# Nine source tiles at a time for the last 53 attention targets

## The chip, the cores and the metric

The kernel runs on one core of a Trainium2 chip. The metric is the device time of one execution in microseconds; the figure of a kernel is the median of its runs. Its engines are named as in the profile: PE (TensorE, with PEld for its weight loads), DVE (VectorE), ACT (ScalarE), POOL (GpSimd) and SP (SyncE, which here issues DMAs).

## The reference

Two graph layers on 3125 nodes with 256 features, each of a graph convolution, a mixing step and an expert step. The change lies in the expert step of the first layer, where a graph attention decides how a node's experts are weighed. Cut to that:

```
h = (x @ W_gat).reshape(M, HEADS, NUM_EXPERTS)        # M = 3125, 4 heads, 4 experts
src = concatenate([edge_index[0], loops])             # edges and a loop at each node
dst = concatenate([edge_index[1], loops])
a_src = (h * att_src).sum(-1)
a_dst = (h * att_dst).sum(-1)
e = leaky_relu(a_src[src] + a_dst[dst], negative_slope=0.2)
e_max = segment_max(e, dst)
ee = exp(e - e_max[dst])
denom = segment_sum(ee, dst)
alpha = ee / (denom[dst] + 1e-16)
agg = segment_sum(h[src] * alpha[:, :, None], dst)    # then layer norm, top 2, softmax
```

## The kernel before

The edges are first made into a dense matrix of counts C in DRAM: row is the target, column the source, and the value is how often the edge occurs. The attention then works on full tiles. For a source tile of 128 nodes (on the partitions) and a group of targets (along the columns) it makes the term exp(e - e_max) for each of four heads, multiplies it by the count, and TensorE sums over the sources with the values h as weights.

Nodes lie in NT = 25 tiles of 128; the last has LAST = 53. Sources are taken tile by tile. Targets are taken in groups of eight tiles (`wide`, L1058): groups 0, 1 and 2 have 1024 targets, group 3 has only the 53 of the last tile. The loop (L1272) takes group 3 first, then 0, 1, 2, and each has 25 steps, one for each source tile.

Before that, a loop over the targets (L1000 to L1039) finds the maxima with VectorE, and from them makes up nine rows of values for each target (`pq`), which are transposed and written to DRAM (`pq_d`, L1039). Rows 0 and 1 hold the slope-1 value of heads 2 and 3 less the maximum. Rows 2, 3 and 6, 7 hold the slope-0.2 value of heads 0, 1 and 2, 3 less the maximum. Rows 4, 5 and 8 hold 0.8 times the target's own value, for heads 0, 1 and 2.

One step has these parts:

- `logits` (L1065): at a group's first step it loads seven rows of `pq_d`, spread over all partitions (`pqb`, L1072), and lets PE spread two more into PSUM (`pb`, L1081). At every second step it loads the counts of two source tiles (`cd`, L1088 or, for the 53, L1092; two buffers). Then the terms before the exponential, in a buffer `ex` of four: for heads 0 and 1 (and head 2 at odd steps) a Relu on ACT (L1099, L1102) and an add on POOL (L1100, L1103), for the others one operation on DVE with `pb` from PSUM (L1105).
- `terms` (L1108): four Exps on ACT, one for each head, with the source's part as a bias (L1116); transposes of the counts on PE into PSUM (`ct`, L1121, two buffers); one DVE operation on all heads, min with 1 and product with the count (L1123).
- `summed` (L1126): four products on PE into `pa` (L1135), a PSUM tile of which there is one buffer.

The loop keeps `logits` one step ahead of `terms`, and `summed` one piece behind. When a group is done, `weighed` (L1138) copies `pa` (L1148), divides, does the layer norm and the choice of experts, and adds the experts' results to `xs`; it is a generator of which the loop takes a piece at a time during the next group, and its small operations run on POOL for groups 3, 0 and 1. The instructions are written in this order, and a planner then decides the order on each engine by priority and readiness, so that some stand elsewhere than they were written; within an engine they run in the planned order.

Of the kernel before, what the change touches and what calls it, by code (L numbers as in the profile page):

```python
# [8 lines left out]
F32 = mybir.dt.float32  # L9
# [8 lines left out]
P = 128  # L18
# [25 lines left out]
HELD = 8  # L44
PACE = 1.05
COLS = 32
MOSTW = 192
CLR = 3056
BEFORE = 4096.0
# [36 lines left out]
def tile_gps(ctx: ExitStack, tc: tile.TileContext, a, out):  # L86
# [43 lines left out]
    A1 = dram.tile([P * CLR * 25], BF16, name="A1")  # L130
    C2 = dram.tile([P * CLR * 25], F32, name="C2")
    as_d = dram.tile([4, N], F32, name="as_d")
    pq_d = dram.tile([9, N], F32, name="pq_d")
    y_d = dram.tile([NT, P, 4, D], F32, name="y_d")
    slots = dram.tile([EX * CAP + SLOT, XW], F32, name="slots")
    hT_d = dram.tile([P, 4, N], F32, name="hT_d")
# [153 lines left out]
    def split_rows(r):  # L290

        return [(0, r)] if r % 16 == 0 else [(0, r - r % 16), (r - r % 16, r)]
# [614 lines left out]
    with ExitStack() as st:  # L907
# [39 lines left out]
        with ExitStack() as st2:  # L947
            ps = st2.enter_context(tc.tile_pool(name="ps_gat", bufs=1, space=PSUM))
            xp = st2.enter_context(tc.tile_pool(name="experts", bufs=1))
            beside0 = experts()  # L950
            ap = st2.enter_context(tc.tile_pool(name="gatp", bufs=1))
            wgat = ap.tile([P, 2, 16], F32, name="wgat", tag="wgat")
            nc.sync.dma_start(wgat, a["w_gat"])
            for g in range(NG):
                ts = tiles_of(g)
                r = rows_of(ts[-1])
                nx = work_rows(len(ts), r)
                normed(nx, [xs[:r, t, :] for t in ts], r, scalar=True)
                hT = work.tile([P, 2, 512], F32, name="hT", tag="hT")
                transposed(ps, hT, nx, r)  # L960
                nc.sync.dma_start(xf_d[:, :, 512 * g:512 * g + cols_of(g)], hT[:, :, :cols_of(g)])
                ph = ps.tile([P, 512], F32, name="ph", tag="pa", bufs=2)
                for j, t in enumerate(ts):
                    for k in range(2):
                        T.matmul(ph[:r, 16 * j:16 * j + 16], lhsT=hT[:, k, j * P:j * P + r], rhs=wgat[:, k, :],
                                 start=(k == 0), stop=(k == 1))
                V.tensor_copy(hg[:r, ts[0]:ts[-1] + 1, :], ph[:r, :16 * len(ts)].rearrange("p (t h) -> p t h", h=16))
            for nm in ("att_src", "att_dst"):
                tmp = ap.tile([P, NT, 16], F32, name="atmp", tag="atmp")
                V.tensor_tensor(tmp, hg, bcast(nm)[:, None, :].to_broadcast([P, NT, 16]), op=OP.mult)  # L970
                V.tensor_reduce(att[nm].rearrange("p t h -> p (t h)"), tmp.rearrange("p t (h e) -> p (t h) e", e=4),
                                axis=AX.X, op=OP.add)

            for g in range(NG):
                p = ps.tile([P, 512], F32, name="tr", tag="tr", bufs=2)
                for j, t in enumerate(tiles_of(g)):
                    r = rows_of(t)
                    T.transpose(p[:4, j * P:j * P + r], att["att_src"][:r, t, :], ident[:r, :r])
                n = cols_of(g)
                asT = ap.tile([4, 512], F32, name="asT", tag="rowsT", bufs=2)  # L980
                S.activation(asT[:, :n], p[:4, :n], AF.Copy)
                nc.sync.dma_start(as_d[:, 512 * g:512 * g + n], asT[:, :n])
            V.tensor_scalar(as8[:, :, 0:2], att["att_src"][:, :, 0:2], 0.8, None, op0=OP.mult)
            V.tensor_scalar(as8[:, :, 2:4], att["att_src"][:, :, 2:4], -0.8, None, op0=OP.mult)
            V.tensor_scalar(as6[:, :, 0:2], att["att_src"][:, :, 0:2], 0.2, None, op0=OP.mult)
            V.tensor_copy(as6[:, :, 2:4], att["att_src"][:, :, 2:4])
            V.tensor_scalar(as2[:, :, 0:1], att["att_src"][:, :, 2:3], 0.8, None, op0=OP.mult)
            V.tensor_scalar(as2[:, :, 1:2], att["att_src"][:, :, 2:3], 0.2, None, op0=OP.mult)
            for _ in range(2):
                next(beside0, None)  # L990
            asb = ap.tile([P, 4, N], F32, name="asb", tag="asb")
            for h in range(4):
                nc.sync.dma_start(asb[:, h, :], as_d[h:h + 1, :].to_broadcast([P, N]))
            edge_stack.close()
            tc.no_sync_barrier()
            rp = ap
            ap = st2.enter_context(tc.tile_pool(name="gat0", bufs=1, reuse_waits="tile"))


            for g in range(NG):  # L1000
                ts = tiles_of(g)
                for t in ts:
                    r = rows_of(t)
                    cnt = ap.tile([P, N], F32, name="cnt", tag="cnt", bufs=2)
                    for q0, q1 in split_rows(r):
                        nc.sync.dma_start(cnt[q0:q1], C22[t * P + q0:t * P + q1, :])
                    for i, (c0, c1) in enumerate(((0, MID), (MID, N))):
                        w = c1 - c0
                        pen = ap.tile([P, MID], F32, name="pen", tag="pen", bufs=2)
                        S.activation(pen[:r, :w], cnt[:r, c0:c1], AF.Relu, scale=MASKED, bias=big[:r])  # L1010
                        for h in range(4):
                            junk = ap.tile([P, MID], F32, name="am", tag="am", bufs=1)
                            V.tensor_tensor_reduce(out=junk[:r, :w], in0=asb[:r, h, c0:c1], in1=pen[:r, :w], scale=1.0,  # L1013
                                                   scalar=-3.0e38, op0=OP.subtract, op1=OP.max,
                                                   accum_out=zz[:r, i, t, h:h + 1])
                    next(beside0, None)

                r, n = rows_of(ts[-1]), cols_of(g)  # L1020
                z0, z1 = (zz[:r, i, ts[0]:ts[-1] + 1, :] for i in range(2))
                zg, ad = z[:r, ts[0]:ts[-1] + 1, :], att["att_dst"][:r, ts[0]:ts[-1] + 1, :]
                m = small.tile([P, 4, 4], F32, name="gm", tag="gm")
                pq = small.tile([P, 4, 9], F32, name="pq", tag="pq")
                k = len(ts)
                V.tensor_tensor(zg, z0, z1, op=OP.max)
                V.tensor_tensor(zg, zg, ad, op=OP.add)
                V.scalar_tensor_tensor(m[:r, :k], zg, 0.2, zg, op0=OP.mult, op1=OP.max)
                V.tensor_tensor(pq[:r, :k, 0:2], ad[:, :, 2:4], m[:r, :k, 2:4], op=OP.subtract)
                V.scalar_tensor_tensor(pq[:r, :k, 2:4], ad[:, :, 0:2], 0.2, m[:r, :k, 0:2], op0=OP.mult, op1=OP.subtract)  # L1030
                V.tensor_scalar(pq[:r, :k, 4:6], ad[:, :, 0:2], 0.8, None, op0=OP.mult)
                V.tensor_scalar(pq[:r, :k, 8:9], ad[:, :, 2:3], 0.8, None, op0=OP.mult)
                V.scalar_tensor_tensor(pq[:r, :k, 6:8], ad[:, :, 2:4], 0.2, m[:r, :k, 2:4], op0=OP.mult, op1=OP.subtract)
                p = ps.tile([P, 512], F32, name="tr", tag="tr", bufs=2)
                for j in range(k):
                    T.transpose(p[:9, j * P:j * P + r], pq[:r, j, :], ident[:r, :r])
                pqT = rp.tile([9, 512], F32, name="pqT", tag="rowsT", bufs=2)
                S.activation(pqT[:, :n], p[:9, :n], AF.Copy)
                nc.sync.dma_start(pq_d[:, 512 * g:512 * g + n], pqT[:, :n])  # L1039
            for _ in beside0:  # L1040
                pass

        with ExitStack() as st2:
            ps = st2.enter_context(tc.tile_pool(name="ps_gat1", bufs=1, space=PSUM))
            ap = st2.enter_context(tc.tile_pool(name="gat1", bufs=1, reuse_waits="tile"))
            def ptile():
                return ps.tile([P, 512], F32, name="ct", tag="ct", bufs=2)
# [78 lines left out]
            def summed(g, s, ex, c, m, state):  # L1126
                ts = wide[g]
                r, rt = rows_of(s), rows_of(ts[-1])
                n = P * (len(ts) - 1) + rt
                if s == 0 and c == 0:  # L1130
                    state["sums"] = ps.tile([P, 1024], F32, name="pa", tag="pa", bufs=1)
                pa = state["sums"]
                for h in range(4):
                    at = 20 * s + 5 * h
                    T.matmul(pa[32 * h:32 * h + 32, c:c + m], lhsT=hgp[:r, at:at + 32], rhs=ex[:r, h, c:c + m],  # L1135
                                 start=(s == 0), stop=(s == NT - 1))

            def weighed(g):  # L1138

# [129 lines left out]
                if want in (None, where):  # L1269
                    want = next(done, "none")  # L1270

            for x in [(g, s) for g in (3, 0, 1, 2) for s in range(NT)] + [None]:  # L1272
                if x:
                    ahead.append(logits(*x, state))
                    if len(ahead) == 1:
# [561 lines left out]
```

## Time and profile before

| | us |
|---|---|
| median of 3 runs | 5010.62 (5009.96 to 5020.74) |
| the profiled execution | 5011.07 |
| its span, first to last instruction | 5009.2 |
| the 53 targets: first Relu to the copy of their sums | 2990.5 to 3037.8 |
| the three full groups: to the copy of the last sums | to 3591.7 |

The profile is of one execution. Busy times are sums over an engine's instructions. In an order of time each row gives the start, the length, the engine, the line, the operation with output and inputs, and in brackets how long the engine was idle before it and what ended that. "x4" means four like instructions merged into a row. In a row of a line or a tile, three durations stand for minimum, median and maximum in ns. In a table by stage each engine has its busy us and its count of instructions, then follow the granted clock of PE, the share of DMA time, and GB/s.

The granted PE clock is 0.50 in both the stretch 2985 to 2991 and the stage of the 53 targets, and 0.76 to 0.94 in the stretches of the full groups from 3042 on. POOL does nothing for 391.1 us before its first add of the attention at 2990.96.

### The profile page before, as it was taken

The numbers are of one execution on the slowest core, as the hardware profiler recorded it, in microseconds if no ns is written. First come the engines' busy times: TensorE is split into PE (matmuls) and PEld (weight loads), VectorE is DVE, ScalarE is ACT, GpSimd is POOL, SyncE is SP. The second block draws the span as 40 slices with busy tenths as digits, with TensorE's granted clock in tenths as the row PEclk, the third lists the DMA queues.
The fourth block names the chain that finished last, engine by engine and source line by source line (L and its number), as shares of the span: only waits on it lengthen the run. The fifth ranks groups of instructions, "written<-read, shape, count | busy, mean of one in ns | idle before, by whom it ended". The sixth has DMA issues, their size and how long they took to land. (4 is left out here: it accounts for less than half of the span.)

```text
span 5009.2 us, 50021 instructions
## 1 busy us (share of the span) xinstructions
PE 3962.3 (79%) x16580; PEld 2289.4 (46%) x16671; DVE 3195.5 (64%) x8087; ACT 1516.3 (30%) x2412; POOL 2723.9 (54%) x1835
## 2 busy tenths in 40 slices
PE   1467788778866786788979955576789998999998
PEld 1244455444543454454456632232345444544477
DVE  7978887888799879511149987989882031321331
ACT  0312132113211131130034449998640030000033
POOL 2578888888888888877750007888520030010033
PEclk6768887888877787889979977887999999999999
DMA  9934443444322322236565533332382212222266
GB/s 331 290 54 69 76 70 43 73 76 63 47 26 17 34 9 22 4 28 119 65 168 191 184 126 100 103 98 72 96 258 70 80 47 65 68 63 61 68 169 164
DMA packets 446884, 472.05 MB, mean 94 GB/s; under 512 B 213042, under 2 KB 354139, under 8 KB 441558
## 3 DMA queue, kind: packets, MB, share of 16 engines
q1 hardware_dynamic: 249418, 455.15, 29.0%
q0 software_dynamic: 197184, 13.47, 12.2%
q8 instruction: 139, 2.28, 0.2%
q14 instruction: 143, 1.16, 0.1%
HBM read 338.77 MB, written 130.63 MB: 94 GB/s over the span
## 5 line engine op out<-in xcount | busy, mean ns | idle before, releaser
L404 POOL DMA_INDIRECT A<-lowa,keya x782 | 1213.8, 1552 | 368.5 <-issue 222.0
L404 POOL DMA_INDIRECT C<-valb,keyb x512 | 793.7, 1550 | 219.8 <-issue 146.1
L1100 POOL TENSOR_TENSOR ex<-ex,pqb 128x1024 f32<-128x1024 f32 (+3 forms) x200 | 366.8, 1856 | 463.6 <-ACT ex L1099 463.4
L350 DVE SCALAR_TENSOR_TENSOR junk<-kr,keya,w_before 128x640 bf16<-128x640 f32 (+2 forms) x729 | 603.5, 828 | 12.2 <-DMA kr<-keys_a 2.0
L393 DVE SCALAR_TENSOR_TENSOR junk<-kr,keyb,w_before 128x1024 bf16<-128x1024 f32 (+1 forms) x390 | 496.4, 1273 | 12.9 <-DMA kr<-keys_b 6.3
L195 PE MATMUL tr<-ident,rows 128*128 128x128 f32 (+1 forms) x500 | 108.4, 371 | 492.6 <-ACT rows L181 486.4
L229 PE MATMUL mm<-hT,w 128*128 128x512 f32 (+1 forms) x896 | 420.2, 634 | 17.2 <-ACT hT L197 17.2
L760 PE MATMUL ag<-chb,Hb 128*128 128x512 bf16 (+1 forms) x1752 | 412.1, 385 | 17.2 <-DMA chb<-A 15.0
L760 PE MATMUL ag<-chb,xb 128*128 128x512 bf16 (+3 forms) x1907 | 398.0, 365 | 15.8 <-DMA chb<-A 13.2
L1013 DVE CUSTOM_DVE_ANT_0 am<-asb,pen 128x1664 f32<-128x1664 f32 (+3 forms) x200 | 357.3, 1786 | 54.0 <-ACT pen L1010 43.7
L717 PE MATMUL o<-w,hid 128*128 128x256 f32 (+1 forms) x1600 | 384.3, 393 | 0.0
L1135 PE MATMUL pa<-ex,hgp 128*32 128x512 f32 (+3 forms) x1400 | 204.5, 664 | 201.6 <-DVE ex L1123 200.4
L1123 DVE SCALAR_TENSOR_TENSOR ex<-ex,ct 128x2048 f32<-128x2048 f32 (+3 forms) x175 | 345.8, 2007 | 27.6 <-ACT ex L1116 14.1
L1116 ACT ACTIVATE ex<-ex,as 128x1024 f32<-128x1024 f32 (+3 forms) x400 | 345.0, 932 | 4.9 <-DVE ex L1105 4.9
L717 PEld LDWEIGHTS o<-w,hid 128*128 128x128 f32 (+1 forms) x1600 | 297.0, 190 | 79.4 <-issue 37.5
L1366 POOL DMA_INDIRECT slots<-rb,r_ati x50 | 50.0, 1000 | 513.6 <-DVE rb L1359 406.9
L232 ACT ACTIVATE hid<-mm,fm 128x512 f32<-128x512 f32 (+1 forms) x336 | 211.0, 631 | 363.5 <-PE mm L229 362.1
L195 PEld LDWEIGHTS tr<-ident,rows 128*128 128x128 f32 (+1 forms) x500 | 68.6, 180 | 538.7 <-ACT rows L181 521.1
L229 PEld LDWEIGHTS mm<-hT,w 128*128 128x128 f32 x896 | 192.0, 233 | 237.6 <-issue 190.4
L760 PEld LDWEIGHTS <-xb 128*128 128x128 bf16 (+1 forms) x2100 | 183.2, 97 | 231.9 <-issue 22.6
L760 PEld LDWEIGHTS <-Hb 128*128 128x128 bf16 (+1 forms) x2100 | 184.1, 99 | 226.6 <-issue 33.2
L181 ACT ACTIVATE rows<-xs,ln_nmr,rs_y 128x256 f32<-128x256 f32 (+1 forms) x225 | 118.9, 592 | 494.8 <-DVE ln_nmr L174 475.5
(441 smaller groups left out, 6653.5 us busy)
## 6 DMA issues: line engine op xcount, KB each, us to landing
C<-zero SPq DMA_DIRECT2D x25, 1528.0 KB
cnt<-C SPq DMA_DIRECT2D x24, 1562.5 KB
cd<-C SPq DMA_DIRECT2D x36, 1024.0 KB
kr<-keys_b SPq DMA_DIRECT2D x64, 512.0 KB
f1w<-in_f_w_dram SPq DMA_DIRECT2D x56, 512.0 KB
slots<-blank SPq DMA_DIRECT2D x15, 1820.0 KB
kr<-keys_a SPq DMA_DIRECT2D x48, 512.0 KB
kr<-keys_a SPq DMA_DIRECT2D x69, 320.0 KB
```

What stands on the lines that cost most here:

```text
L229: T.matmul(ph[:, :n], lhsT=w1[:, k, hb * P:(hb + 1) * P], rhs=xT[:, k, :n], start=(k == 0), stop=(k == 1))
L232: S.activation(h[:, :n], ph[:, :n], AF.Gelu, bias=bias[hb])
L350: V.scalar_tensor_tensor(junk[:, :k * P], self.kr[:, at:at + k * P], key[:, c + j:c + j + 1], self.w_before[:, u:u + k * P], op0=OP.is_equ ...
L393: V.scalar_tensor_tensor(out, kk, key[:, c + j:c + j + 1], by, op0=OP.is_equal, op1=OP.mult, accum_out=more[:, j:j + 1] if i else self.val ...
L404: s = G.indirect_dma_start(out=self.flat, out_offset=bass.IndirectOffsetOnAxis(ap=self.idx[:, c:c + 1], axis=0), in_=(self.val if self.low ...
L717: T.matmul(po[:r], lhsT=hid[hb][:, j * P:j * P + r], rhs=w2[:, hb, :], start=(hb == 0), stop=False)
L760: T.matmul(acc[fb, g][:, :n], lhsT=Xb[:r, s, i, fb * P:(fb + 1) * P], rhs=ch[:r, at:at + n], start=first, stop=last, skip_group_check=g == ...
L1013: V.tensor_tensor_reduce(out=junk[:r, :w], in0=asb[:r, h, c0:c1], in1=pen[:r, :w], scale=1.0, scalar=-3.0e38, op0=OP.subtract, op1=OP.max, ...
L1100: G.tensor_tensor(e, e, pq[:r, h, :n], op=OP.add)
L1116: S.activation(ex[:r, h, :n], ex[:r, h, :n], AF.Exp, bias=sc)
L1123: V.scalar_tensor_tensor(e4, e4, 1.0, ct[:r, None, :m].to_broadcast([r, 4, m]), op0=OP.min, op1=OP.mult)
L1135: T.matmul(pa[32 * h:32 * h + 32, c:c + m], lhsT=hgp[:r, at:at + 32], rhs=ex[:r, h, c:c + m], start=(s == 0), stop=(s == NT - 1))
```

## The change

The 53 targets leave the loop and get a function of their own, `last_targets`. It takes the source tiles in groups of MANY = 9 (9, 9 and 7) and makes the terms of a group together, with the columns in the order source tile, target. For each head three DVE operations replace Relu, add and L1105: 0.8 times the source's value plus 0.8 times the target's; max with zero plus the target's slope-0.2 row; plus 0.2 times the source's value. The source's value is read from `att_src`, repeated over the 53 columns; the target's rows, `rows4`, are repeated over the source tiles. One Exp without a bias works on all four heads of a group. The counts of all source tiles are loaded in two pieces (of 2048 and 1077 columns) that hold both `cd` buffers until they are transposed. The min and product is one DVE operation a head, in the last group two, since its last source tile has 53 rows. The products on PE are as before. `pq` has ten rows instead of nine (the tenth is head 3's 0.8 row). The loop then starts at group 0, with `weighed(3)` handed to it as the work to be taken in pieces.

```
-                pq = small.tile([P, 4, 9], F32, name="pq", tag="pq")
+                pq = small.tile([P, 4, 10], F32, name="pq", tag="pq")
...
-                V.tensor_scalar(pq[:r, :k, 8:9], ad[:, :, 2:3], 0.8, None, op0=OP.mult)
+                V.tensor_scalar(pq[:r, :k, 8:10], ad[:, :, 2:4], 0.8, None, op0=OP.mult)
...
+            def last_targets():
+
+                n, q0 = LAST, P * (NT - 1)
+                rows4 = ap.tile([P, 8, LAST], F32, name="rows4", tag="rows4")
+                for i, k in enumerate((2, 6, 4, 8)):
+                    nc.sync.dma_start(rows4[:, 2 * i:2 * i + 2, :], pq_d[k:k + 2, q0:N].rearrange("(o k) n -> o k n", o=1)
+                                      .to_broadcast([P, 2, n]))
+                cds = []
+                for c0 in range(0, N, 8 * SRC):
+                    c1 = min(c0 + 8 * SRC, N)
+                    cd = ap.tile([P, 8, SRC], F32, name="cd", tag="cd", bufs=2).rearrange("p j c -> p (j c)")
+                    for p0, p1 in split_rows(n):
+                        nc.sync.dma_start(cd[p0:p1, :c1 - c0], C22[q0 + p0:q0 + p1, c0:c1])
+                    cds.append(cd)
+                state["sums"] = ps.tile([P, 1024], F32, name="pa", tag="pa", bufs=1)
+                pa = state["sums"]
+                for s0 in range(0, NT, MANY):
+                    some = list(range(s0, min(s0 + MANY, NT)))
+                    k = len(some)
+                    ex = ap.tile([P, 4, 1024], F32, name="ex", tag="ex", bufs=4)
+                    e = ex.rearrange("p h n -> p (h n)")[:, :4 * k * n].rearrange("p (h s n) -> p h s n", h=4, n=n)
+                    for h in range(4):
+                        src = att["att_src"][:, s0:s0 + k, h:h + 1].to_broadcast([P, k, n])
+                        w, a8 = (rows4[:, i + h:i + h + 1, :].to_broadcast([P, k, n]) for i in (0, 4))
+                        V.scalar_tensor_tensor(e[:, h], src, 0.8, a8, op0=OP.mult, op1=OP.add)
+                        V.scalar_tensor_tensor(e[:, h], e[:, h], 0.0, w, op0=OP.max, op1=OP.add)
+                        V.scalar_tensor_tensor(e[:, h], src, 0.2, e[:, h], op0=OP.mult, op1=OP.add)
+                    S.activation(e, e, AF.Exp)
+                    ct = ptile()
+                    for j, s in enumerate(some):
+                        r, c = rows_of(s), P * s
+                        T.transpose(ct[:r, j * n:j * n + n], cds[c // (8 * SRC)][:n, c % (8 * SRC):c % (8 * SRC) + r],
+                                    ident[:n, :n])
+                    full = k - (some[-1] == NT - 1)
+                    for r, i0, i1 in ((P, 0, full), (LAST, full, k)):
+                        if i0 < i1:
+                            for h in range(4):
+                                V.scalar_tensor_tensor(e[:r, h, i0:i1], e[:r, h, i0:i1], 1.0,
+                                                       ct[:r, i0 * n:i1 * n].rearrange("p (s n) -> p s n", n=n),
+                                                       op0=OP.min, op1=OP.mult)
+                    for j, s in enumerate(some):
+                        r = rows_of(s)
+                        for h in range(4):
+                            at = 20 * s + 5 * h
+                            T.matmul(pa[32 * h:32 * h + 32, :n], lhsT=hgp[:r, at:at + 32], rhs=e[:r, h, j, :],
+                                     start=(s == 0), stop=(s == NT - 1))
...
-            for x in [(g, s) for g in (3, 0, 1, 2) for s in range(NT)] + [None]:
+            last_targets()
+            done = weighed(3)
+            for x in [(g, s) for g in (0, 1, 2) for s in range(NT)] + [None]:
```

More of the change, by code (lines that the diff above doesn't have):

```diff
@@ L46 @@
 COLS = 32
+MANY = 9
 MOSTW = 192
@@ L132, in tile_gps @@
     as_d = dram.tile([4, N], F32, name="as_d")
-    pq_d = dram.tile([9, N], F32, name="pq_d")
+    pq_d = dram.tile([10, N], F32, name="pq_d")
     y_d = dram.tile([NT, P, 4, D], F32, name="y_d")
@@ L1035, in tile_gps @@
                 for j in range(k):
-                    T.transpose(p[:9, j * P:j * P + r], pq[:r, j, :], ident[:r, :r])
-                pqT = rp.tile([9, 512], F32, name="pqT", tag="rowsT", bufs=2)
-                S.activation(pqT[:, :n], p[:9, :n], AF.Copy)
+                    T.transpose(p[:10, j * P:j * P + r], pq[:r, j, :], ident[:r, :r])
+                pqT = rp.tile([10, 512], F32, name="pqT", tag="rowsT", bufs=2)
+                S.activation(pqT[:, :n], p[:10, :n], AF.Copy)
                 nc.sync.dma_start(pq_d[:, 512 * g:512 * g + n], pqT[:, :n])
```

## The prediction

> **What bounds the kernel now.** I read the page's busy table first, then the stage of the change in the table by stage, then its waits and its order of time, then the costs of single operations by form.
>
> ```profile
> PE 3962.3 (79%) x16580; PEld 2289.4 (46%) x16671; DVE 3195.5 (64%) x8087; ACT 1516.3 (30%) x2412; POOL 2723.9 (54%) x1835
> ```
>
> ScalarE (ACT) is the least busy engine of the whole span, but the attention is another matter. Its second part, 2991 to 3592 us, cut where the group of 53 ends:
>
> ```profile
> core 0: us, PE busy (x) PEld busy (x) DVE busy (x) ACT busy (x) POOL busy (x), PEclk, DMA share, GB/s
> 2991.00:3028.00 37.00, 16.41 (x203) 9.32 (x204) 17.22 (x61) 36.91 (x156) 16.68 (x62) 0.50 0.31 111
> 3028.00:3592.00 564.00, 366.10 (x2052) 140.47 (x2051) 511.53 (x394) 514.13 (x514) 466.90 (x261) 0.84 0.31 98
> ```
>
> In the first row ACT works 36.91 of 37.00 us and VectorE (DVE) 17.22: the 53 targets are bound by ACT. In the second row both stand at 91%, so a lead that one of them alone wins is soon used up. The waits of the first stretch say the same: DVE's L1123 waits for ACT's Exp, 19 times.
>
> ```profile
> DVE ex L1123 <- ACT ex L1116: 7.8, 19, 1.7
> PE ct L1121 <- DMA cd<-C: 3.3, 1, 3.3
> ```
>
> By form, the widths of the 53 and of the full groups:
>
> ```profile
> L1116 ACT ACTIVATE ex<-ex,as x400: 323/1132/1150, 2993.1 to 3583.0; 128x1024 f32<-128x1024 f32 x96, 128x53 f32<-128x53 f32 x32, 53x1024 f32<-53x1024 f32 x4, 53x53 f32<-53x53 f32 x2
> L1123 DVE SCALAR_TENSOR_TENSOR ex<-ex,ct x175: 361/2278/2290, 2994.2 to 3588.2; 128x2048 f32<-128x2048 f32 x144, 128x212 f32<-128x212 f32 x24, 53x2048 f32<-53x2048 f32 x6, 53x212 f32<-53x212 f32 x1
> ```
>
> The minimum is the 53's. An Exp of 53 columns costs 323 ns against 1132 for 1024: 279 ns of it are fixed. 25 tiles with 6.5 ACT instructions each, at 0.23 us apart, are the 37 us. Where the stage ends and what follows:
>
> ```profile
> 2990.53 1.03 ACT L1099 ACTIVATE ex<-pqb,as 128x53 f32<-128x53 f32 x4 [5.22 <-DMA pqb<-pq_d]
> 3034.54 2.47 DVE L1105 SCALAR_TENSOR_TENSOR ex<-pqb,as,pb 128x1024 f32<-128x1024 f32 x2 [5.54 <-PE pb L1081]
> 3042.22 4.48 DVE L1123 SCALAR_TENSOR_TENSOR ex<-ex,ct 128x2048 f32<-128x2048 f32 x2 [0.16 <-ACT ex L1116]
> ```
>
> The mark I measure against is 3042.22, the first L1123 of the first full group (group 0, source tile 0). What that instruction gains, the end should gain: after it 75 equal steps follow, then stages that depend on their end.
>
> [...] 896 elements, both sources in SBUF, 1.09 us (row below[...]). [...]
>
> ```profile
> 18.73 1.09 DVE L278 SCALAR_TENSOR_TENSOR kfa<-sfa,dfa 128x896 f32<-128x896 f32 x1
> ```
>
> [...] The trace shows such a lock. A VectorE operation on 16 elements took 2.47 us and ended with a GpSimd (POOL) add of 2.37 us; a two-SBUF one on 4 elements took 0.64 beside an add of 0.65:
>
> ```profile
> 3088.01 2.47 DVE L1214 TENSOR_SCALAR g_over<-g_diff 53x16 f32<-53x16 f32 x1
> 3088.10 4.67 POOL L1100 TENSOR_TENSOR ex<-ex,pqb 128x1024 f32<-128x1024 f32 x2
> 3660.99 1.30 POOL L732 TENSOR_TENSOR rest<-rows,xb 128x256 f32<-128x256 f32 x2 [0.99 <-ACT xb L731]
> 3661.04 0.64 DVE L174 SCALAR_TENSOR_TENSOR ln_nmr<-ln_mv,rs_y 128x4 f32<-128x4 f32 x1
> ```
>
> The kernel before keeps one operand of L1105 and L1123 in PSUM, so its adds run free. The new operations have both in SBUF. [...]
>
> **The change, part by part.** *Removed:* for the 53, all ACT work (36.9 us), POOL's adds, L1105 and the 25 small L1123; the transposes and the 100 products per source tile and head stay. ACT keeps three Exps of 1908, 1908 and 1484 elements[...], so 32 us of ACT go. The wait of 3.3 us for counts goes too: all counts are asked for at once (0.66 MB) and are needed 8 us later.
>
> *Added on VectorE.* Groups of 9, 9 and 7 source tiles. The A part: three operations per head, 12 a group. [...] Dependent ones in the trace stand 0.03 us more than their duration apart (0.26 for 0.23), independent ones about 0.06 less: 0.66 and 0.55 on average. 24 x 0.66 + 12 x 0.55 = 22.4 us. The B part, min and product, has its counts in PSUM. L1123's 212 elements at 0.38 and 2048 at 2.28 give 1.035 ns each, so 477 at 0.65, 0.59 apart: 8 x 0.59 = 4.7. The last group is 4 of 318 (0.43) and 4 of 53 (0.15): 2.3. Together 29.4 us against 17.2 now. VectorE is the stage's bound then.
>
> *The start.* Four small loads (rows4) in place of one; at 0.38 us an issue the fourth is 1.1 us later on SP's queue, but the first head needs the first and third: I take 2990.8 in place of 2990.53. The four count loads follow, then group 0's rows (3584 KB), issued at 2988.9 now and landed near 3002 by the DMA bars; 2 us later on SP costs nothing before 3003.
>
> *The waits.* B of a group waits for its Exp, behind it in program order the next group's A. But instructions aren't kept in program order: the timeline shows a load of the weighing stage (L1233) at 2947.61, in the maxima loop, and layer-norm steps of the next stage between the last L1123s at 3580. So I take A of the next group into the Exp's time. Only the last Exp [...] has no A left; two L1105 of group 0 (2.5 us) fill it. The end of B: 2990.8 + 29.4 + 2.5 = 3022.7. PE's products take 0.35 us a source tile, and its `pb` for group 0 (3.8 us) can run early, both beside that.
>
> *Brought forward.* ACT and POOL are now free from 3003 on, and ex has four buffers: three groups take three, the fourth goes to tile 0 of group 0; tile 1 takes the first group's once its products are done (about 3006), tile 2 the second's (about 3016). So two, three and two Relus and as many POOL adds can come early; ACT is then far enough ahead that tile 0's Exps are done at 3022. Without interference the mark moves from 3042.2 to 3022.7: 19.5 us.
>
> *The lock.* Each POOL add inside an A part stops VectorE for up to 2.37 us. At least 2 fall there, at most 7. I take 4: two of tile 0, and of tile 1's three two, since its third Relu stands on ACT behind the second Exp, which the delayed A holds up. 4 x 2.37 = 9.5.
>
> *Nothing:* one row more in pq (L1024 to L1038): the same instruction counts. The held count buffers are free by the third group's transposes, before group 0 is in need.
>
> **Sum:** 19.5 - 9.5 = 10.0 us. The profiled execution took 5011.07 (span 5009.2 and 1.9 around it), so 5001.1; against the median 5010.62, 5000.6.
>
> **Rivals.**
> - *Fewer collisions.* POOL loses the lock to back-to-back VectorE, or only tile 0's adds come early: 19.5 less 0 to 4.7, so 4991 to 4996. For it: an add waits as well as VectorE. Against: at 3088 POOL won.
> - *Small gain.* Program order is kept: per group A 7.9, Exp and hand-over 2.0, B 2.4, so 12.3 twice and 10.6: end at 3026; then products 3.0, `pb` 3.8, two L1105 2.5 and an Exp 1.3: mark at 3036.6, gain 5.6, 5005.0. Six or seven adds in the A parts give the same, 2.9 to 5.3. Against the first: the rows moved across stages.
> - *Slower: the second SBUF operand.* [...] It decides once rate and lock together cost over 19.5 us. L278 speaks against the rate, though not with an operand repeated across columns as here.
>
> **Numbers.** Chances: forecast 0.42 (three to five adds, gain 7.6 to 12.4), fewer collisions 0.22, small gain 0.22, slower 0.14. The bound of what can be told from no change is 0.2%, 10.0 us. Faster by more: 0.22 and a bit over half of the forecast's, 0.46. Within: 0.18 + 0.22 + 0.03 = 0.43. Slower by more: 0.11 of the last. The range 4989 to 5016 takes in all cases but most of the last.
>
> **What would show it.** In the changed profile: twelve new VectorE operations a group at 0.65 us ([...] near 3 beside an add is the lock); [...] VectorE's next A inside each Exp (else the second rival); POOL adds of 1024 before the last B, and how many; the first full L1123 near 3032 from an unchanged start of the stage. The forecast is wrong if that mark gains and the end does not, the full groups then being limited by something that the lead doesn't help.

## The result and the profile after

| | before | after |
|---|---|---|
| median of 20 runs each on one chip, us | 5018.69 (5009.96 to 5025.64) | 5001.20 (4991.77 to 5016.90) |
| ratio | | 0.9966, 95% interval 0.9959 to 0.9973 |
| the profiled execution, us | 5011.07 | 4992.12 |
| its span, us | 5009.2 | 4990.4 |

The change makes the kernel faster by 0.34%, some 17 us (14 to 21 by the interval). Of the two profiled executions each lies near the low end of its kernel's runs, so they can be compared. Lines up to L1137 have moved by one at most: L1105, L1116, L1123, L1135 and L1148 of before are now L1106, L1117, L1124, L1136 and, further down, L1196. The new function stands at L1139 to L1184: L1163 to L1165 are the three VectorE operations of a head (the A part), L1166 is the Exp, L1176 min and product (the B part).

The busy table of the page of after:

```profile
PE 3960.1 (79%) x16667; PEld 2282.4 (46%) x16667; DVE 3210.0 (64%) x8076; ACT 1483.3 (30%) x2253; POOL 2710.7 (54%) x1773
```

ScalarE has lost 33.0 us of work (1516.3 to 1483.3), VectorE has gained 14.5. The table by stage, cut again into the 53 targets and the full groups:

```profile
core 0: us, PE busy (x) PEld busy (x) DVE busy (x) ACT busy (x) POOL busy (x), PEclk, DMA share, GB/s
2992.00:3029.00 37.00, 15.16 (x235) 10.34 (x233) 35.96 (x57) 13.85 (x13) 12.28 (x5) 0.55 0.80 275
3029.00:3582.00 553.00, 366.36 (x2012) 137.74 (x2012) 506.75 (x387) 503.70 (x498) 455.19 (x255) 0.83 0.27 89
```

In the first row the bound has changed hands: VectorE is busy for 35.96 of 37.00 us, where ScalarE had 36.91. Of these 35.96 us 5.0 are a standstill, shown below, and ScalarE's 13.85 already hold Relus and Exps of group 0. The full groups look as before, both engines near 91%.

By form, durations in ns as minimum, median and maximum:

```profile
L1163 DVE SCALAR_TENSOR_TENSOR ex<-att_src,rows x12: 533/649/2686, 2993.0 to 3017.2; 128x477 f32<-128x477 f32 x8, 128x371 f32<-128x371 f32 x4
L1164 DVE SCALAR_TENSOR_TENSOR ex<-ex,rows x12: 530/646/651, 2994.2 to 3020.3; 128x477 f32<-128x477 f32 x8, 128x371 f32<-128x371 f32 x4
L1166 ACT ACTIVATE ex<-ex x3: 1440/1793/1794, 3000.0 to 3021.7; 128x1908 f32<-128x1908 f32 x2, 128x1484 f32<-128x1484 f32 x1
```

The medians, 0.65 us for 477 columns with both operands in SBUF and one of them repeated, are near what two rows of before come to: L278's 1.09 us for 896 elements, at L1123's 1.035 ns an element, gives 0.66, and 0.55 for 371 columns. The maximum of L1163, 2686 ns for 371 columns that otherwise take 533, is something else, and the order of time of all engines shows what (PE's rows left out):

```profile
3008.98 1.79 ACT L1166 ACTIVATE ex<-ex 128x1908 f32<-128x1908 f32 x1 [7.24 <-DVE ex L1165]
3009.78 0.99 DVE L1164 SCALAR_TENSOR_TENSOR ex<-ex,rows 128x371 f32<-128x371 f32 x2
...
3010.68 3.21 ACT L1100 ACTIVATE ex<-pqb,as 128x1024 f32<-128x1024 f32 x3
...
3011.15 2.32 DVE L1176 SCALAR_TENSOR_TENSOR ex<-ex,ct 128x477 f32<-128x477 f32 x4
3011.90 7.58 POOL L1101 TENSOR_TENSOR ex<-ex,pqb 128x1024 f32<-128x1024 f32 x3 [408.86 <-ACT ex L1100]
...
3013.39 1.28 DVE L1165 SCALAR_TENSOR_TENSOR ex<-att_src,ex 128x371 f32<-128x371 f32 x1
3014.59 5.28 DVE L1163 SCALAR_TENSOR_TENSOR ex<-att_src,rows 128x371 f32<-128x371 f32 x2
3019.80 0.98 DVE L1164 SCALAR_TENSOR_TENSOR ex<-ex,rows 128x371 f32<-128x371 f32 x2
3020.71 0.99 DVE L1165 SCALAR_TENSOR_TENSOR ex<-att_src,ex 128x371 f32<-128x371 f32 x2
...
3021.73 1.44 ACT L1166 ACTIVATE ex<-ex 128x1484 f32<-128x1484 f32 x1 [7.84 <-DVE ex L1165]
...
3026.07 3.65 DVE L1106 SCALAR_TENSOR_TENSOR ex<-pqb,as,pb 128x1024 f32<-128x1024 f32 x3
...
3029.78 2.29 DVE L1124 SCALAR_TENSOR_TENSOR ex<-ex,ct 128x2048 f32<-128x2048 f32 x1
```

Three POOL adds follow one another from 3011.90 to 3019.48. Beside the first, VectorE's B part takes 2.32 us for four, as it does at 3003.23 without an add: its counts come from PSUM. Then come operations with both sources in SBUF: one takes 1.28 in place of 0.53, two take 5.28 in place of 0.99, and behind the last add two take 0.98 again. That is 0.75 + 4.29 = 5.0 us of standstill, and the last Exp comes later by it (ScalarE is idle for 7.84 us before it). The first full-width L1124, the mark, is at 3029.78.

Where the time went, from three profiled executions of each kernel. All figures are us, counted from the last copy of `pqT`, with which the stage begins; "rest" is from the last copy of `num` to the end of the span.

| | before | after |
|---|---|---|
| last copy of pqT | 2985.1, 2987.9, 2989.5 | 2986.1, 2988.2, 2986.2 |
| first operation of the 53 | 5.4 (first profile) | 7.0 (first profile) |
| the mark | 57.1, 57.5, 57.5 | 43.7, 43.8, 43.5 |
| last copy of num | 606.6, 608.5, 610.3 | 595.6, 596.2, 595.5 |
| rest | 1417.5, 1421.2, 1417.7 | 1408.7, 1413.7, 1417.0 |
| span | 5009.2, 5017.6, 5017.5 | 4990.4, 4998.1, 4998.7 |

By the means the mark gains 13.7 us, the attention's end 12.7, and the rest 5.7, although ScalarE, VectorE, POOL and the DMA queue work through the same instructions in the same order there (PE's records are a little incomplete).

### The profile page after: what moved, and what is told of

Its sections match the earlier page's. It is cut to its first block, busy times and chain, and to the rows that moved or that the text cites. A ratio compares the mean times of both kernels' runs of the same rounds, so it can differ in the third digit from the quotient of the medians.

```text
span 4990.4 us, 49776 instructions
## 1 busy us (share of the span) xinstructions
PE 3960.1 (79%) x16667; PEld 2282.4 (46%) x16667; DVE 3210.0 (64%) x8076; ACT 1483.3 (30%) x2253; POOL 2710.7 (54%) x1773
## 3 DMA queue, kind: packets, MB, share of 16 engines
q14 instruction: 140, 1.15, 0.1%
## 5 line engine op out<-in xcount | busy, mean ns | idle before, releaser
L1101 POOL TENSOR_TENSOR ex<-ex,pqb 128x1024 f32<-128x1024 f32 (+1 forms) x150 | 353.7, 2380 | 466.9 <-ACT ex L1100 466.8
L761 PE MATMUL ag<-chb,xb 128*128 128x512 bf16 (+2 forms) x1950 | 400.1, 365 | 13.6 <-DMA chb<-A 13.1
L1136 PE MATMUL pa<-ex,hgp 128*32 128x512 f32 (+1 forms) x1200 | 202.8, 755 | 176.1 <-DVE ex L1124 175.9
L1124 DVE SCALAR_TENSOR_TENSOR ex<-ex,ct 128x2048 f32<-128x2048 f32 (+1 forms) x150 | 336.4, 2278 | 8.0 <-PE ct L1122 6.0
L1117 ACT ACTIVATE ex<-ex,as 128x1024 f32<-128x1024 f32 x300 | 319.8, 1134 | 2.7 <-DVE ex L1106 2.6
```

The costliest lines, as they stand in the source:

```text
L761: T.matmul(acc[fb, g][:, :n], lhsT=Xb[:r, s, i, fb * P:(fb + 1) * P], rhs=ch[:r, at:at + n], start=first, stop=last, skip_group_check=g == ...
L1101: G.tensor_tensor(e, e, pq[:r, h, :n], op=OP.add)
L1117: S.activation(ex[:r, h, :n], ex[:r, h, :n], AF.Exp, bias=sc)
L1124: V.scalar_tensor_tensor(e4, e4, 1.0, ct[:r, None, :m].to_broadcast([r, 4, m]), op0=OP.min, op1=OP.mult)
```

## The experiments

Ratios are to the kernel before on the same chip, with 95% intervals. Times in the stage are counted as in the table above.

**Ten rows alone.** The kernel before with the tenth row in `pq` and `pq_d`, and nothing else of the change.

```
-                pq = small.tile([P, 4, 9], F32, name="pq", tag="pq")
+                pq = small.tile([P, 4, 10], F32, name="pq", tag="pq")
...
-                V.tensor_scalar(pq[:r, :k, 8:9], ad[:, :, 2:3], 0.8, None, op0=OP.mult)
+                V.tensor_scalar(pq[:r, :k, 8:10], ad[:, :, 2:4], 0.8, None, op0=OP.mult)
```

> The kernel before with ten rows in pq and pq_d and nothing else of the change. After the attention, the changed kernel took 1408.7 us from the last copy of the sums to its end and the kernel before 1417.5, though both issue the same instructions there. Theory: that difference is the scatter between executions; then this kernel is within 3 us of the kernel before, and 1412 to 1422 us from the last copy to the end. Rival: the tenth row moves every DRAM tile that lies behind it, and that is worth some 7 us; then it takes 1407 to 1411 us after the last copy, and its ratio is 0.998 to 0.999.

Ratio 1.0003 (0.9995 to 1.0010); the mark at 57.4, the attention's end at 607.5, the rest 1421.6. The row has no cost that can be measured, and it isn't what shortens the rest.

**A fence behind the 53.** Nothing of group 0 may be planned before the end of `last_targets`.

```
             last_targets()
+            tc.no_sync_barrier()
             done = weighed(3)
```

> The changed kernel with a fence for the planner behind the 53 targets, so that nothing of group 0 is planned ahead of them. Theory: work brought forward is worth more than the lock takes. Without it the 53's last min and product ends at some 34 us after the start of the stage (the last copy of pqT), 6 us sooner than in the changed kernel since no add is in the way, but Relus, adds and pb of group 0 come after it, so that the first full min and product stands at 47 us in place of 43.7, and the kernel is 3 to 7 us slower than the changed one (ratio to before 0.9972 to 0.9980). Rival: the lock takes all of it back; then the ratio is 0.9966 or less.

Ratio 0.9964 (0.9950 to 0.9977), the mark at 47.3, but the attention's end at 591.4, earlier than in the changed kernel (595.8). No add of group 0 lies in an A part any more, and `pb` is late: the order of time of this kernel has VectorE idle for 8.22 us before the four L1106 that precede the mark.

```profile
3036.70 4.86 DVE L1106 SCALAR_TENSOR_TENSOR ex<-pqb,as,pb 128x1024 f32<-128x1024 f32 x4 [8.22 <-PE pb L1082]
3041.50 4.49 DVE L1124 SCALAR_TENSOR_TENSOR ex<-ex,ct 128x2048 f32<-128x2048 f32 x2
```

The ratio is the rival's, though its interval just reaches the theory's 0.9972. A later mark doesn't mean a later end.

**Adds held back.** The first POOL adds of group 0 wait until the last group's terms are made; the order on the engines is that of the changed kernel.

```
+            def late(g, s, add):
+                for o in state["made"][-4:] if g == 0 and s < 3 else []:
+                    tc.add_manual_dep(add.ins, o.ins.name, Edges.after, reason="after the last group's terms")
...
-                        G.tensor_tensor(e, e, pq[:r, h, :n], op=OP.add)
+                        add = G.tensor_tensor(e, e, pq[:r, h, :n], op=OP.add)
+                        late(g, s, add)
...
-                        V.scalar_tensor_tensor(e[:, h], src, 0.2, e[:, h], op0=OP.mult, op1=OP.add)
+                        part = V.scalar_tensor_tensor(e[:, h], src, 0.2, e[:, h], op0=OP.mult, op1=OP.add)
+                        state["made"] = state.get("made", []) + [part]
```

> The changed kernel with the POOL adds of group 0's first three source tiles waiting for the last group's third VectorE operations; the order on every engine is as in the changed kernel. Theory: the three adds inside the A part held VectorE for 5.0 us (1.28 for 0.45 and 5.28 for 0.99), so all A operations now take 0.45 to 0.65 us, the third Exp starts 5 us sooner, the first full min and product stands at 38 to 40 us after the last copy of pqT in place of 43.7, and the kernel gains 3 to 5 us on the changed one (ratio to before 0.9956 to 0.9960). Rival: the adds are needed as soon as VectorE is done, and starting them 5 us later costs as much; then the mark gains 2 us or less and the kernel is as the changed one, 0.9966.

The order of time of this kernel, VectorE and POOL (L1169 and L1171 are L1163 and L1165, L1130 is the mark):

```profile
3024.53 1.00 DVE L1169 SCALAR_TENSOR_TENSOR ex<-att_src,rows 128x371 f32<-128x371 f32 x2
3025.45 1.00 DVE L1170 SCALAR_TENSOR_TENSOR ex<-ex,rows 128x371 f32<-128x371 f32 x2
3026.36 1.00 DVE L1171 SCALAR_TENSOR_TENSOR ex<-att_src,ex 128x371 f32<-128x371 f32 x2
...
3035.44 4.48 DVE L1130 SCALAR_TENSOR_TENSOR ex<-ex,ct 128x2048 f32<-128x2048 f32 x2
```

```profile
3027.58 9.35 POOL L1105 TENSOR_TENSOR ex<-ex,pqb 128x1024 f32<-128x1024 f32 x4 [415.53 <-DVE ex L1171]
```

Without an add beside them, the same instructions that took 5.28 us take 1.00. The mark moves to 38.4, by 5.3 us, as much as the standstill was. The attention ends at 591.6 (4.2 us earlier than the three profiles' mean), and the ratio is 0.9960 (0.9945 to 0.9975), which can't be told from that of the change. The lock is shown, and its price at the mark is 5 us.

**Rows spread by PE.** No `rows4` loads: PE spreads the eight rows from `pqT`, which gets a buffer of its own for the last targets, into the free half of `pa` in PSUM.

```
-                rows4 = ap.tile([P, 8, LAST], F32, name="rows4", tag="rows4")
-                for i, k in enumerate((2, 6, 4, 8)):
-                    nc.sync.dma_start(rows4[:, 2 * i:2 * i + 2, :], pq_d[k:k + 2, q0:N].rearrange("(o k) n -> o k n", o=1)
-                                      .to_broadcast([P, 2, n]))
...
+                rows4 = pa[:, 512:512 + 8 * n].rearrange("p (i n) -> p i n", n=n)
+                for i, row in ((4, 4), (0, 2), (5, 5), (1, 3), (6, 8), (2, 6), (7, 9), (3, 7)):
+                    T.matmul(rows4[:, i, :], lhsT=ident[:10, row:row + 1].to_broadcast([10, P]), rhs=pqT[:, :n],
+                             start=True, stop=True)
```

> The changed kernel with the 53's eight rows spread by eight products on PE from the SBUF copy of pqT into the idle half of pa, in place of the way by DRAM and four loads. Theory: VectorE stood idle for 6.4 us until the rows landed; now it starts some 2 us after the copy in place of 7.0, and two of three operations have an operand in PSUM that no add can lock. The first full min and product stands 5 to 8 us sooner (36 to 39 us after the copy), the kernel gains as much: ratio to before 0.9950 to 0.9957. Rival: the start is not what holds group 0, because its rows (3584 KB) land no sooner and the adds then fall on the third operations as before; then the 53 end sooner, but the mark gains under 2 us, and the ratio stays at 0.9962 to 0.9966.

The terms begin 4.0 us after the copy in place of 7.0, yet the mark is at 43.1, the attention's end at 601.8, and the ratio 0.9966 (0.9952 to 0.9979). The rows now lie in the tile into which PE sums, and the next group's terms wait for PE's products of the group before:

```profile
3002.46 0.65 DVE L1164 SCALAR_TENSOR_TENSOR ex<-att_src,pa 128x477 f32<-128x477 f32 x1 [1.89 <-PE pa L1184]
```

The 3 us at the start were given back by such waits (two of 1.89 us), and two groups' terms no longer overlap the Exp. The terms of the last seven source tiles meet POOL's adds again, and the lock is choosy among their operations:

```profile
3020.29 0.53 DVE L1164 SCALAR_TENSOR_TENSOR ex<-att_src,pa 128x371 f32<-128x371 f32 x1
3020.74 1.78 DVE L1166 SCALAR_TENSOR_TENSOR ex<-att_src,ex 128x371 f32<-128x371 f32 x1
```

Those with the rows from PSUM take 0.53 us beside the adds, those with both inputs in SBUF 1.72 to 1.78. The late end of the attention isn't explained by this stage: this kernel copies the sums of group 0 at 216.6 and of group 1 at 409.6, before the changed kernel does (226.8 and 414.2), and loses this lead in target group 2, which takes 192.2 us in place of 181.5. What it does there was not followed up. So the question of the start stayed open until the rows had a tile of their own (below).

**Both kernels again, for their stages.** Unchanged code; the second profile of each is in the table above.

> The changed kernel once more, for a second profile and a second ratio. Between the profiles so far, the stretch from the copy of the last sums of the attention to the end took 1408.7 us after the change and 1417.5 before, at 0.97 to 0.99 against 0.96 to 0.98 of granted PE clock in the stretch that PE fills. Theory A (the attention alone gained, and the rest is the clock that one execution happens to get): this stretch falls anywhere between 1408 and 1422 us here. Rival B (the rest gains by the change itself): it takes 1407 to 1411 again. Both: ratio 0.9960 to 0.9972; attention's end 594 to 598 us after the last copy of pqT.

> The kernel before once more, for a second profile of it. Theory A (the rest is the clock that the execution gets): the stretch from the copy of the last sums to the end is anywhere between 1408 and 1422 us. Rival B (it is a matter of the program): 1416 to 1419 again. Both: attention's end 605 to 609 us after the last copy of pqT, the first full-width min and product 56 to 58 us after it.

The ratio came out at 0.9966 (0.9955 to 0.9977) again. The rest took 1413.7 and 1421.2 us, both outside what rival B said, so it isn't a fixed property of the program.

**Both repairs together.** The rows in a tile of their own in PSUM (one of the two `ct`), and the adds held back. The lines are shown against the kernel with the rows in `pa`.

```
-                rows4 = pa[:, 512:512 + 8 * n].rearrange("p (i n) -> p i n", n=n)
+                rows4 = ptile()[:, :8 * n].rearrange("p (i n) -> p i n", n=n)
...
+                        late(g, s, add)
```

> The changed kernel with the 53's eight rows spread by PE into one of the two ct tiles in PSUM instead of by DMA, and with the first adds of POOL held until the last group's terms are made. The start of the terms should move from 7.0 to 3.3 us after the last copy of pqT, and no operation of the terms should wait for POOL. Theory that start and lock are what the stage still loses: the first full-width min and product at 34 to 37 us after pqT (43.7 in the changed kernel), attention's end at 587 to 591, ratio to the kernel before 0.9945 to 0.9962. Rival (the full groups give the lead back, since both VectorE and ScalarE are near full there): the mark moves as said, the attention's end stays at 591 to 597, ratio 0.9960 to 0.9972.

The terms begin 4.0 us after the copy, the mark is at 36.3 and the attention's end at 590.2, all but the start within the first theory's figures. Ratio 0.9958 (0.9944 to 0.9972): against the change's 0.9966 that is no difference that can be measured. What is late next is POOL: held back, its adds make an Exp of group 0 wait (1.15 us), and that Exp the mark (1.70). In the order of time of this kernel:

```profile
3022.03 9.35 POOL L1106 TENSOR_TENSOR ex<-ex,pqb 128x1024 f32<-128x1024 f32 x4 [414.09 <-DVE ex L1172]
...
3026.76 3.48 ACT L1124 ACTIVATE ex<-ex,as 128x1024 f32<-128x1024 f32 x3 [1.15 <-POOL ex L1106]
3027.94 4.48 DVE L1131 SCALAR_TENSOR_TENSOR ex<-ex,ct 128x2048 f32<-128x2048 f32 x2 [1.70 <-ACT ex L1124]
```

**One Exp for each head.** Twelve Exps in place of three.

```
-                    S.activation(e, e, AF.Exp)
+                    for h in range(4):
+                        S.activation(e[:, h], e[:, h], AF.Exp)
```

> The changed kernel with four Exps for each group of source tiles, one for each head, in place of one: 12 instead of 3. Theory that VectorE bounds the stage: ScalarE has 23 us of 37 free, so the 9 added fixed costs (some 0.2 us each, 1.7 us) lie in its idle time; the first full-width min and product 42 to 45 us after the last copy of pqT, ratio 0.9960 to 0.9972. Rival (the one Exp for all heads is what gained): 1.7 us or more of the gain is lost at the mark, 45.4 us or later, and the ratio is 0.9970 to 0.9980.

Ratio 0.9964 (0.9951 to 0.9978): the single Exp is not what gains. The twelve take 6.6 us by the order of time, the three took 5.0. The mark came at 39.5, earlier than the theory had it. The planner now puts the Relus of group 0 behind the first two Exps of the last group, so POOL's first add starts as the last A operations do, and nothing stands still. All of this kernel's engines but PE, in order of time:

```profile
3019.35 2.17 ACT L1100 ACTIVATE ex<-pqb,as 128x1024 f32<-128x1024 f32 x2
...
3020.57 10.27 POOL L1101 TENSOR_TENSOR ex<-ex,pqb 128x1024 f32<-128x1024 f32 x4 [412.40 <-ACT ex L1100]
3020.64 0.98 DVE L1165 SCALAR_TENSOR_TENSOR ex<-att_src,ex 128x371 f32<-128x371 f32 x2
```

POOL is the one that waits here: its four adds take 10.27 in place of some 9.35. And the attention ends at 596.7, no earlier than with the mark at 43.7.

**Other sizes of a group.** MANY = 1 and MANY = 3.

```
-MANY = 9
+MANY = 1
```

> The changed kernel with one source tile a group in place of nine (MANY = 1): 300 operations of 53 columns make the terms on VectorE, 100 the min and product, and 25 Exps of 212. Operations of 477 columns stand 0.565 us apart in the changed kernel, those of 371 0.455: 1.04 ns a column and 0.070 us fixed. Theory that the grouping pays these fixed costs once for nine tiles: 0.125 us each, 37.5 + 12.5 = 50 us in place of 25.5, the first full-width min and product some 25 us later, at 66 to 75 us after the last copy of pqT (57 in the kernel before), and the kernel not faster than before, ratio 1.000 to 1.004. Rival (that ScalarE is relieved is what counts, whatever the size): the mark stays below 50, ratio 0.996 to 0.998.

> The changed kernel with three source tiles a group (MANY = 3): operations of 159 columns, by the same sum 0.235 us apart. Terms 96 x 0.235 + 12 x 0.125 = 24.1 us (19.0 with nine), min and product 8.0 (6.5). Fixed-cost theory: the first full-width min and product 6 to 7 us later than with nine, 49 to 52 us after the last copy of pqT, ratio 0.9965 to 0.9990. Rival (size does not matter): 42 to 46, ratio 0.9960 to 0.9972.

With one tile a group: the mark at 66.8, the attention's end at 625.6, ratio 1.0017 (1.0009 to 1.0025), slower than before. With three: 48.7 (0.3 short of what was expected), 598.2, ratio 0.9980 (0.9971 to 0.9989). The stage of MANY = 1 by its table:

```profile
2996.00:3057.00 61.00, 28.23 (x235) 18.46 (x233) 59.33 (x407) 19.43 (x36) 11.36 (x5) 0.50 0.48 167
```

ScalarE is as free as in the change, and VectorE works 59.33 of 61 us, for the same elements in 407 instructions. The lock is no rival here: one operation of the terms was held by an add, for 2.39 in place of 0.21 us. Moving the terms off ScalarE does not pay by itself; making nine tiles' terms in one instruction does.

**Both kernels a third time**, for the third column of the table.

> The changed kernel a third time, for its stages. Theory that the stretch after the attention differs only by how often PE falls to half clock in an execution: 1408 to 1422 us; that the change itself shortens it: below 1414, as 1408.7 and 1413.7 so far. Attention's end 594 to 598 us after the last copy of pqT.

> The kernel before a third time, for its stages. Theory that the stretch after the attention differs only by how often PE falls to half clock in an execution: 1408 to 1422 us; that the change itself shortens it: above 1416, as 1417.5 and 1421.2 so far. Attention's end 605 to 610 us after the last copy of pqT.

The rest took 1417.0 and 1417.7 us, and the kernel before ended its attention at 610.3, 0.3 later than expected. With 1408.7, 1413.7 and 1417.0 the rest of the changed kernel alone spans 8 us.

## Why the prediction was right, and where it was not

That the time agrees, 5000.6 forecast and 5001.2 measured, is luck. The forecast started from a median of three runs, 5010.62; over 20 runs the kernel before has 5018.69, 8.1 us more. The change in time was forecast at -10.0 us and is -17 (-14 to -21). The two errors cancel. The mechanism was right: the bound moves to VectorE, VectorE's work for the 53 is less than ScalarE's was, and POOL's adds take part of the gain. Several terms of the sum were not:

- *The bound.* ScalarE to VectorE, as said. The three Exps, without a bias, took 1.79, 1.79 and 1.44 us. From 1908 and 1484 elements that is 0.83 ns an element and 0.20 us fixed; the Exps of before, with a bias, have the same 0.83 and 0.28 fixed (323 ns for 53 elements, 1132 for 1024). In the 36.9 us of ScalarE before, the forecast's count of instructions misses an ACT_TABLE_LOAD of 1.28 us, amid the work of the engine that bounds the stage. In the changed kernel it comes while ScalarE has nothing else to do. The first row is of before, the second of after:

```profile
2991.81 1.28 ACT L1116 ACT_TABLE_LOAD   x1
2986.29 1.28 ACT L1166 ACT_TABLE_LOAD   x1
```

- *The start*, put 0.3 us later than before, is 1.6 later (7.0 after the copy against 5.4): VectorE waits for the landing of `rows4` (idle for 6.44 us before its first operation). Rows spread by PE remove 3 us of it.
- *The A part* was put at 22.4 us, by an estimate of 0.66 a piece on the average of dependent and independent operations. The planner set two heads' operations side by side, so that all stand 0.565 and 0.455 us apart: 24 x 0.565 + 12 x 0.455 = 19.0. *The B part*: 7.0 forecast, 6.5 measured.
- *Brought forward.* ScalarE and POOL were to start on group 0 from 3003, with seven Relus and adds. ScalarE instead stands idle for 7.24 us before the second Exp, and only behind it, from 3010.68, come three Relus. So only three adds could meet the terms.
- *The lock* was put at four adds of 2.37, 9.5 us. Three came, and they cost 5.0. The first of the three lay beside the B part, which reads PSUM and runs on (0.64 us an operation, as without an add), and held the L1165 behind it for 0.75; the other two cost some 2.1 each. This term is the largest that was mis-sized, and the kernel with the adds held back confirms its size.
- *Left out* were the three L1106 of group 0 that VectorE does between the last min and product and the mark (3026.07, 3.65 us; 3.7 from start to start). The forecast had two such operations, in the time of the last Exp, and put the mark right behind the end of the B part.
- *The mark* was to come 47.1 us after the copy in the first profile (57.1 less 10.0) and came at 43.7. Start +1.3, A part -3.4, B part -0.5 and lock -4.5 would be 7.1 sooner; the 3.7 left out bring it to 3.4. By the means the mark gained 13.7 us, not 10.0, between the forecast and the rival of fewer collisions (14.8 to 19.5).
- *What the mark gains, the end should gain.* On the average of three profiles that held: 13.7 at the mark, 12.7 at the attention's end. As a rule it fell: with a fence the mark is 3.6 us later than in the change and the end 4.4 earlier, and with twelve Exps the mark is 4.2 earlier and the end 0.9 later (one profile each; three of the changed kernel end within 0.7 us of each other). A likely reading is that ScalarE and VectorE are both near full in group 0 (169.3 and 163.7 us busy of the 183.1 from the mark to the copy of its sums in the changed kernel), and that what counts is how much of its work both have behind them, of which the mark shows one instruction; no run tests it.
- *The rest* was left as it is. It is 5.7 us shorter on average, a third of the 19 us between the mean spans of the table. So that part of the measured gain is not one that the forecast explains.
- *The slower rival*: a second SBUF operand costs no rate here. 477 columns take 0.65 us with both operands in SBUF (L1163) and 0.64 with one of them in PSUM (L1176).
- *The small gain*, program order kept: VectorE's next A does run inside the first two Exps, as the order of time shows for the second (3008.98 beside L1164).

What stays open is why the rest is shorter. The clock records of the traces know only the full and the half clock of PE. In the four profiles with the attention of before the rest is 1417.5 to 1421.6 us, in the ten with the 53's terms on VectorE it is 1408.6 to 1420.7, with means of 1419.5 and 1414.0. In the rest of the four, PE is at half clock for 116 to 123 us, in nine of the ten for 92 to 111. The tenth, with the rows in `pa`, has some 130 us and the longest rest of the ten. So the length goes with the half clock, not with the kernel alone. Whether the half clock makes the rest longer or longer waits bring on the half clock, and whether the change makes it rarer or ten and four executions fell so, the runs don't settle.

## What to carry to other kernels

An engine can be relieved of many small instructions by another if that one takes them in large pieces: here 36 operations of up to 477 columns cost 19 us, where 300 of 53 took more time than was saved (ratio 1.0017). Before moving work to VectorE, ask which of its operands lie in SBUF and what POOL is doing then; the place of three adds decides 5 us here, and an operand in PSUM whether an operation is held (0.53 us beside adds with one, 1.72 to 1.78 with both in SBUF). And a gain at one instruction isn't yet a gain at the end where two engines are near full: measure at the end of the stage, in several executions.

## What the hardware showed that was not expected

PE's clock in one and the same program. In the sums over `Hb` the same 19 products take 4.28 us in one execution of the changed kernel and 7.16 in another. The first, in PE's order of time, and its 20 us in the table by stage, with a granted clock of 1.00:

```profile
4478.30 4.28 PE L761 MATMUL ag<-chb,Hb 128*128 128x512 bf16 x19
```

```profile
4470.00:4490.00 20.00, 18.14 (x93) 9.83 (x92) 11.75 (x69) 2.75 (x7) 0.49 (x1) 1.00 0.10 27
```

The second execution, same instructions, with 0.83, and 0.50 in a part of it:

```profile
4483.85 7.16 PE L761 MATMUL ag<-chb,Hb 128*128 128x512 bf16 x19
```

```profile
4473.00:4493.00 20.00, 18.71 (x85) 10.26 (x84) 10.66 (x66) 1.94 (x4) 0.00 (x0) 0.83 0.10 27
4483.00:4489.70 6.70, 6.70 (x18) 2.89 (x19) 4.50 (x30) 0.23 (x1) 0.00 (x0) 0.50 0.00 0
```

The stage of the sums over `Hb` took 501.1, 504.8 and 506.1 us in three executions of the changed kernel, with 20.5, 23.9 and 27.3 us at half clock by the traces' clock records. Products of this form stand 0.216 us apart at the full clock and 0.427 at the half clock in the trace of before. So the 6.8 us more are worth 3.4 of the 5.0 at most, and in the kernel before, 504.0, 507.5 and 504.7 us go with 30.7, 27.3 and 30.7. So the clock is part of the spread there, not all of it. What brings the clock down here, no run shows: before the half clock of the second execution PE's longest idle in 20 us was 1.29 us, and the first execution has one of 1.30 too and keeps the full clock.

The lock between VectorE and POOL works both ways: POOL holds VectorE in the changed kernel (2.69 us for a 0.53 us operation), and with twelve Exps POOL's adds take longer beside VectorE's operations (10.27 us for four that take 9.35 with the adds held back). By the single records the three held operations of the changed kernel, at 3013.39, 3014.59 and 3017.20, start after the adds that they lie beside (3011.90, 3014.22, 3016.84). With twelve Exps the first add starts at 3020.57, and the two L1165 that start behind it, at 3020.64, take their usual 0.98. And at 3088.01 of the kernel before the held operation starts 0.09 us ahead of the add. So the recorded start doesn't tell which of the two is held, and what decides is open. An operand in PSUM was enough to escape the lock in every case shown here: 0.64 us for the B part's operations beside an add, 0.53 for those that read `pa`, and in the kernel before, where L1105 and L1123 read PSUM, at most 1.28 and 2.29, with medians of 1.27 and 2.28. But an operation needn't have two inputs in SBUF to be held: the forecast's own row at 3088.01, 2.47 us, is an operation with one tile as input.
